# Four smaller transfers for the decays, and fewer, re-ordered rows for the reciprocals, in a gated linear-attention block

## The chip, the cores and the metric

The kernel runs on one core of one Trainium2 chip. A core has TensorE (PE, matrix products; its weight loads are listed as PEld), VectorE (DVE), ScalarE (ACT), GpSimd (POOL) and SyncE (SP), each with its own queue of instructions, and 16 DMA engines that all queues share. The metric is the device time of the program in microseconds (us), lower is better. The times shown are medians of runs. A profile is one execution, recorded by the hardware.

## The reference

The block has a linear attention with decays and a mixture of experts, each behind a layer norm whose scale and shift come from a condition `c`. There are 8 sequences of 2048 tokens, 256 features, 16 heads of 64, and 8 experts of which each token uses 2. Cut to what matters here:

```python
h = layernorm(x) * (1 + ca) + sa
q, k = elu(h @ Wq) + 1, elu(h @ Wk) + 1          # 16 heads of 64
v, a = h @ Wv, sigmoid(h @ Wa + ba + 2)          # one decay per head and token
S = a * S + k v^T                                # step by step over the tokens
z = a * z + k
o = (q S) / (q z + eps)                          # division by one number per head and token
x = x + ga * (o @ Wo)
h = layernorm(x) * (1 + cb) + sb
x = x + gb * mixture_of_two_experts(h)
```

Two quantities of this are what the change handles: the decays `a` as sums of logarithms per head and token, and the reciprocal of `q z + eps`, also one number per head and token.

## The kernel before

**Tiling.** A group is 256 tokens of one sequence; there are 64 groups. Each has two chunks of 128 tokens. Within a chunk the attention is computed as a masked matrix product (`Chunk.scores`, L486, and `Chunk.outputs`, L557); between chunks a state `S` is carried (`from_state`, `state`). All matrices are float32.

**Order.** The program order is written out by hand in a loop over the groups (L1158 on, under `manual_schedule`). One pass of it handles four groups at once: `here` has its attention outputs computed, `ahead` its keys, queries and decays, `coming` its norms and decay sums, `prev` its routing to the experts. Expert tiles (128 rows gathered for one expert: `load`, `turn`, `apply`, L846 to L891) are put in between by `expert_tiles`. Each engine does its instructions in that order, and a DMA queue issues in that order as well. Nearly all plain DMAs are issued by SP, on one queue (q1); POOL issues the indirect ones (L757 scatters rows to the experts' lists, L990 gathers the experts' results back).

**Decays.** `decays` (L343) makes for each head and token the running sum of the logarithm and its exponential, and stores both in DRAM (`led`, L374), as well as the decay itself (`ad`, L380). `chunk_decays` (L400) brings them back spread over the partitions: `dec` is a tile of 128 partitions by 16 heads by 128 tokens; each partition gets the same 16 x 128 numbers, 8 KB, in one DMA (L405). Then `el` gets half of the heads on each half of the partitions (`spread_pairs`, L392). POOL fills the part of `dec` above the diagonal with 1e30 (L409), and ScalarE makes exponentials of it, four heads between two other steps (L415). There are two `dec` buffers. The loop brings in chunk 0 of `ahead` early in a pass (L1212) and chunk 1 at its end (L1342).

**Reciprocals.** `denominators` (L444) multiplies the running sums `zz` (already times the queries) by a selecting matrix, so that head pair `2g+u`, half `q`, ends in row `32 g + 2 (q xor u) + u` of a PSUM tile of 128 rows by 256 tokens. 16 of the 128 rows are used. VectorE adds epsilon and takes reciprocals of all 128 (L457, L458). The whole tile is stored to DRAM (`rdd`, L460, 128 rows of 1 KB), and two DMAs (L465), one per half of the partitions, spread the used rows to 64 partitions each; of every block of 32 rows they read two neighbouring ones, 2 KB, so a partition's 8 KB come in four pieces. `Chunk.outputs` multiplies the product in PSUM by these (L577), for each `u` with a stride of two head pairs in `rb`. The denominators of `ahead` are made in the pass before the one that uses them: the store and the spread stand near the end of a pass, with `at` (the decays spread for the key sums, two DMAs of 512 KB, L395), `dec` of chunk 1 and `el` around them. In SP's order this stretch reads: `rdd`, `at` twice, `dec`, `rb` twice, `el` twice.

**Semaphores.** SP's DMAs use eight semaphores in turn, and each DMA first waits until the one that used its semaphore before, eight DMAs earlier, has landed.

Of the kernel before, what the change touches and what calls it, by code (L numbers as in the profile page):

```python
# [8 lines left out]
F32 = mybir.dt.float32  # L9
# [4 lines left out]
P = 128  # L14
C = 128
G = 2
GT = G * C
DH = 64
# [12 lines left out]
def adaln_block_kernel(  # L31
# [17 lines left out]
    nc = tc.nc  # L49
    B, N, D = x.shape  # L50
    F = wq.shape[1]
    H = F // DH
# [17 lines left out]
    dram = ctx.enter_context(tc.tile_pool(name="dram", bufs=3, space=bass.MemoryType.DRAM))  # L70
# [7 lines left out]
    def small_tile(name):  # L78
        return big_tile(name).rearrange("p i t -> p (i t)")
# [18 lines left out]
    for e in range(E):  # L98
# [6 lines left out]
        out=before, in_=before, compare_op=ALU.is_gt, fill=0.0, base=0,  # L105
# [45 lines left out]
    with tc.tile_pool(name="early", bufs=1) as early:  # L151
        wmod_sb = early.tile([P, KD, 4, D], F32, tag="wmod_sb", name="wmod_sb")
        for n in range(2):
            for k in range(KD):
                nc.scalar.dma_start(
                    out=wmod_sb[:, k, 2 * n : 2 * n + 2, :], in_=wmod_v[:, k, n, 0:2, :]
# [5 lines left out]
        for n, which in enumerate((0, 1, 3, 4)):  # L162
            t = cpool.tile([P, KD, B], F32, tag=f"modT{which}", name=f"modT{which}")
# [60 lines left out]
    for r in range(2 * G):  # L224
        row = (r // 2) * 32 + (r % 2) * NP
        nc.sync.dma_start(
            out=bias_a[row : row + NP, :],
            in_=ba.rearrange("(j q o) -> q j o", q=2, o=1)[r % 2],
# [7 lines left out]
    for u in range(2):  # L236
        for q in range(2):
            half = q ^ u
            nc.scalar.dma_start(
                out=wo_sb[half * DH : (half + 1) * DH].rearrange("p (g u) f -> p g u f", u=2)[  # L240
                    :, :, u, :
                ],
                in_=wo_v[u, q],
# [148 lines left out]
    def spread_pairs(dst, src):  # L392

        for q in range(2):
            nc.sync.dma_start(  # L395
                out=dst[q * DH : (q + 1) * DH],
                in_=src[q * NP : (q + 1) * NP].partition_broadcast(DH),
            )

    def chunk_decays(led, x, ch):  # L400

        tag = f"{x.tag}_{ch}"
        dec = wk2.tile([P, H, C], F32, tag="dec", name=f"dec_{tag}", bufs=2)
        el = wk2.tile([P, NP, C], F32, tag="el", name=f"el_{tag}", bufs=2)
        nc.sync.dma_start(out=dec, in_=led[0, ch * 32 : ch * 32 + H, :].partition_broadcast(P))  # L405
        yield dec, el
        spread_pairs(el, led[1, ch * 32 : ch * 32 + H, :])
        yield
        nc.gpsimd.affine_select(  # L409
            out=dec, in_=dec, compare_op=ALU.is_ge, fill=1e30, base=0,  # L410
            pattern=[[0, H], [1, C]], channel_multiplier=-1,
        )
        yield
        for h in range(H):
            nc.scalar.activation(  # L415
                dec[:, h, :], dec[:, h, :], AF.Exp, scale=-1.0, bias=x.lt[:, 0, ch, h : h + 1]
            )
            if h % 4 == 3:
                yield
# [24 lines left out]
    def denominators(qT, zz, tag):  # L444

        pd = small_tile(f"pd_{tag}")
        for u in range(2):
            for g in range(4):
                nc.tensor.matmul(  # L449
                    pd[g * 32 : (g + 1) * 32, :GT],  # L450
                    sel[:, u, :],
                    zz[:, 2 * g + u, :],
                    start=(u == 0),
                    stop=(u == 1),
                )
        rd = wk2.tile([P, GT], F32, tag="rd", name=f"rd_{tag}", bufs=1)
        nc.vector.tensor_scalar(rd, pd[:, :GT], ATTN_EPS, None, ALU.add)  # L457
        nc.vector.reciprocal(rd, rd)  # L458
        rdd = dram.tile([P, GT], F32, tag="rdd", name=f"rdd_{tag}")
        nc.sync.dma_start(out=rdd, in_=rd)  # L460
        yield

        rb = wk2.tile([P, NP, GT], F32, tag="rb", name=f"rb_{tag}", bufs=1)
        for half in range(2):
            nc.sync.dma_start(  # L465
                out=rb[half * DH : (half + 1) * DH].rearrange("p (g u) t -> p g (u t)", u=2),
                in_=rdd.rearrange("(g r) t -> g r t", r=32)[:, 2 * half : 2 * half + 2, :]
                .rearrange("g r t -> g (r t)")
                .partition_broadcast(DH),
            )  # L470
        yield rb

    class Chunk:
# [83 lines left out]
        def outputs(self, u):  # L557

            po = self.po[u]
            for i in range(NP // 2):  # L560
                for half in range(2):
                    j = 2 * i + u
                    q = half ^ u
                    h = 2 * j + q
                    nc.tensor.matmul(  # L565
                        po[half * DH : (half + 1) * DH, i, :],
                        self.v[:, h * DH : (h + 1) * DH],
                        self.dec[:, q * NP + j, :],
                        start=(self.S is None and i == 0),
                        stop=True,  # L570
                        skip_group_check=True,
                    )

            def pairs(t):
                return t.rearrange("p (g u) t -> p g u t", u=2)[:, :, u, :]

            nc.vector.tensor_mul(pairs(self.oT), po, pairs(self.group.rb[:, :, self.tok]))  # L577

        def decay_state(self):
            if self.last:  # L580
# [576 lines left out]
    with tc.manual_schedule():  # L1157
        for n in range(-2, total + 1):  # L1158
# [52 lines left out]
            if ahead:  # L1211
                dk = chunk_decays(ahead.led, ahead, 0)  # L1212
                ahead.dec_el[0] = next(dk)
                next(dk)
                kp = project(ahead.hT, "k", ahead.tag)
                ahead.kT = next(kp)
                zk = key_sums(ahead.kT, ahead.at, None if ahead.g == 0 else z, ahead.tag)
                zz, z = next(zk)
# [15 lines left out]
            if prev:  # L1234
# [4 lines left out]
                if n - 1 == dense_from:  # L1239

                    for e in range(0, E, 4):
                        for k in range(KD):
                            nc.sync.dma_start(
                                out=(wq_sb, wk_sb)[e // 4][:, k, :].rearrange(
                                    "p (e f) -> p e f", f=D
                                ),
                                in_=ew_d[e : e + 4, :, k, :].rearrange("e p f -> p e f"),
# [3 lines left out]
                else:  # L1251
                    u = unit_of[n - 1]
# [63 lines left out]
            if ahead:  # L1316
                dn = denominators(ahead.qT, zz, ahead.tag)
# [23 lines left out]
            if ahead:  # L1341
                ahead.dk = chunk_decays(ahead.led, ahead, 1)  # L1342
                ahead.dec_el[1] = next(ahead.dk)
                ahead.rb = next(dn)
                next(ahead.dk)
# [17 lines left out]
            if here and n < dense_from:  # L1363
                u = unit_of[n]
                if units[u] is None:
                    units[u] = Unit(u)
                nc.sync.dma_start(
                    out=units[u].xd[here.g * GT : (here.g + 1) * GT, :].rearrange(
                        "(c p) d -> p c d", p=P
                    ),  # L1370
                    in_=here.xt,
# [50 lines left out]
```

## Time and profile before

| | |
|---|---|
| median of 3 runs | 3899.13 us (3888.24 to 3919.3) |
| the profiled execution's own time | 3885.85 us |
| its span, first to last instruction | 3884.1 us |
| mean granted TensorE clock | 0.969 of full speed |
| bytes moved by DMA | 712.09 MB, mean 183 GB/s |
| of these on SP's queue | 625.52 MB in 313488 packets |
| `dec` (L405) | 128 DMAs of 1024 KB |
| `at` / `el` (L395) | 128 DMAs of 512 KB / 256 of 256 KB |
| `rdd` (L460) / `rb` (L465) | 64 DMAs of 128 KB / 128 of 512 KB |

A profile line of the waits names who waited, for whom, the total in us, how often, and the longest. A line of the timeline has start, duration, engine, source line, operation, output and inputs, shapes, how many instructions were merged, and in brackets the idle time before with what ended it. PE's idle time is what can be won as long as its work stays the same. A pass of the loop takes 50 us in the first sequence, 53 to 64 us in the middle, where expert tiles run beside the attention, and up to 84 us in the last sequence, in which more expert tiles are put between.

### The profile page before, as it was taken

What the parts mean: (1) busy time and instruction counts of PE and PEld (TensorE: products, weight loads), DVE (VectorE), ACT (ScalarE), POOL (GpSimd) and SP (SyncE); (2) the same over time, 40 slices, a digit from 0 to 9 for tenths busy, and PEclk for the clock granted to TensorE, in tenths of its full rate; (3) what the DMA queues carried; (4) which work ended last, traced back from release to release, by engine and by line L of the source; (5) the groups of instructions that cost most, each with busy time, mean ns of one, the idle gap of its engine ahead of it and who ended that gap; (6) DMA issues with size and microseconds to landing.
All of it is one profiled execution on the core that took longest, in us unless ns stands there. A gap on an engine that the chain in (4) does not pass through costs nothing.

```text
span 3884.1 us, 82134 instructions
## 1 busy us (share of the span) xinstructions
PE 3546.7 (91%) x28998; PEld 2742.2 (71%) x28998; DVE 2640.0 (68%) x6396; ACT 2083.2 (54%) x5423; POOL 1846.2 (48%) x1986
## 2 busy tenths in 40 slices
PE   5999999999999999999999998999999999788786
PEld 3777777777777777777777776777777777666665
DVE  3777777777667667667766767767767767556555
ACT  3555555655555645655555655555655555444442
POOL 1444443443555454454545546445455444444554
PEclk9999999999999999999999999999999999989898
DMA  6444457666676666676576676576576576666766
GB/s 188 130 122 133 133 148 194 196 176 170 196 217 175 186 179 193 182 216 185 161 222 188 181 192 188 172 209 190 171 209 195 164 205 180 200 190 197 212 199 189
DMA packets 347404, 712.09 MB, mean 183 GB/s; under 512 B 43736, under 2 KB 212968, under 8 KB 322416
## 3 DMA queue, kind: packets, MB, share of 16 engines
q1 hardware_dynamic: 313488, 625.52, 57.5%
q0 software_dynamic: 27264, 74.49, 5.6%
q10 hardware_dynamic: 6240, 6.84, 0.6%
q8 instruction: 229, 3.75, 0.4%
q14 instruction: 183, 1.50, 0.1%
HBM read 577.29 MB, written 132.53 MB: 183 GB/s over the span
## 4 chain that ended last, share of the span: by engine, by line
PE 64%; DVE 15%; ACT 7%; issue 6%; DMA 3%; POOL 2%; SPq 0%; another core or an unknown queue 0%; DVEq 0%; ACTq 0%; POOLq 0%
PE pv L528 10%; PE pw L615 9%; PE pq L326 7%; PE pk L326 7%; PE po L565 6%; PE py L886 5%; PE sc L492 4%; PE ps L599 3%; PE po L548 3%; DVE at L433 3%; PE pd L449 2%; PE pk L511 2%; DMA xg<-xrows 2%; POOL at L1154 2%; ACT dec L415 2%
## 5 line engine op out<-in xcount | busy, mean ns | idle before, releaser
L415 ACT ACTIVATE dec<-dec,lt 128x128 f32<-128x128 f32 x2048 | 628.5, 389 | 14.2 <-POOL dec L409 14.2
L1154 POOL TENSOR_TENSOR at<-at,qT 128x512 f32<-128x512 f32 x256 | 326.1, 1285 | 579.2 <-DVE rmark L715 401.6
L326 PE MATMUL pk<-hT_a,wk_sb 128*128 128x256 f32 x2048 | 512.8, 395 | 5.0 <-issue 4.7
L326 PE MATMUL pq<-hT_a,wq_sb 128*128 128x256 f32 x2048 | 482.2, 389 | 13.2 <-DVE kT L338 12.5
L615 PE MATMUL pw<-wo_sb,oT 128*128 128x256 f32 x2048 | 478.0, 388 | 4.7 <-DVE oT L577 4.7
L528 PE MATMUL pv<-wv_sb,hT_a 128*128 128x512 f32 x1024 | 472.3, 604 | 2.5 <-DVE yg L890 2.3
L326 PEld LDWEIGHTS pq<-hT_a,wq_sb 128*128 128x128 f32 x2048 | 392.0, 194 | 75.4 <-DVE kT L338 19.4
L875 ACT ACTIVATE xgT<-pxt,modT,modT 128x128 f32<-128x128 f32 x622 | 245.0, 447 | 358.4 <-PE pxt L870 336.6
L615 PEld LDWEIGHTS pw<-wo_sb,oT 128*128 128x128 f32 x2048 | 393.5, 195 | 59.2 <-DVE oT L577 5.5
L326 PEld LDWEIGHTS pk<-hT_a,wk_sb 128*128 128x128 f32 x2048 | 381.1, 196 | 70.3 <-issue 13.3
L886 PE MATMUL py<-we,xgT 128*128 128x256 f32 x1244 | 348.4, 405 | 62.1 <-ACT xgT L875 28.3
L409 POOL TENSOR_SCALAR_AFFINE_SELECT dec<-dec 128x2048 f32<-128x2048 f32 x128 | 256.9, 2007 | 266.4 <-DMA dec<-led 201.8
L577 DVE TENSOR_TENSOR oT<-po,rb 128x512 f32<-128x512 f32 x256 | 173.1, 690 | 296.2 <-PE po L565 119.2
L433 DVE TENSOR_TENSOR_SCAN at<-at,z,kT 128x256 f32<-128x256 f32 x448 | 353.7, 830 | 2.0
L501 DVE TENSOR_TENSOR dec<-sc,dec 128x512 f32<-128x512 f32 x512 | 327.3, 682 | 36.8 <-PE sc L492 35.2
L528 PEld LDWEIGHTS pv<-wv_sb,hT_a 128*128 128x128 f32 x1024 | 189.8, 192 | 216.7 <-issue 174.2
L620 POOL TENSOR_TENSOR xt<-xt,dx 128x256 f32<-128x256 f32 x128 | 94.3, 737 | 480.2 <-DVE dx L619 479.9
L565 PE MATMUL po<-dec,v 128*64 128x128 f32 x4096 | 272.3, 278 | 36.1 <-issue 26.0
L886 PEld LDWEIGHTS py<-we,xgT 128*128 128x128 f32 x1244 | 227.5, 200 | 103.6 <-ACT xgT L875 35.7
L492 PE MATMUL sc<-qT,kT 64*128 64x128 f32 x4096 | 298.1, 286 | 0.1
L492 PEld LDWEIGHTS sc<-qT,kT 64*128 64x128 f32 x4096 | 250.1, 188 | 63.0 <-issue 62.8
L336 ACT ACTIVATE lowk<-pk 128x512 f32<-128x512 f32 x256 | 152.3, 595 | 257.0 <-PE pk L326 218.8
(199 smaller groups left out, 6208.2 us busy)
## 6 DMA issues: line engine op xcount, KB each, us to landing
dec<-led SPq DMA_DIRECT2D x128, 1024.0 KB
we<-ew_d SPq DMA_DIRECT2D x311, 384.0 KB
at<-ad SPq DMA_DIRECT2D x128, 512.0 KB
el<-led SPq DMA_DIRECT2D x256, 256.0 KB
rb<-rdd SPq DMA_DIRECT2D x128, 512.0 KB
xg<-xrows SPq DMA_DIRECT2D x311, 128.0 KB
yrows<-yg SPq DMA_DIRECT2D x311, 128.0 KB
xt<-in_L_attn_x_dram SPq DMA_DIRECT2D x64, 256.0 KB
```

The costliest lines, as they stand in the source:

```text
L326: nc.tensor.matmul(pp[:, j * GT : (j + 1) * GT], w[:, k, (jj + j) * P : (jj + j + 1) * P], hT[:, k, :], start=(k == 0), stop=(k == KD - 1),)
L409: nc.gpsimd.affine_select(out=dec, in_=dec, compare_op=ALU.is_ge, fill=1e30, base=0, pattern=[[0, H], [1, C]], channel_multiplier=-1,)
L415: nc.scalar.activation(dec[:, h, :], dec[:, h, :], AF.Exp, scale=-1.0, bias=x.lt[:, 0, ch, h : h + 1])
L433: nc.vector.tensor_tensor_scan(zz[:, j, :], at[:, j, :], kT[:, j, :], 0.0 if z is None else z[:, j : j + 1], ALU.mult, ALU.add,)
L492: nc.tensor.matmul(sc[q][:, i, :], self.kT[rows, half * 4 + i, self.tok], self.qT[rows, half * 4 + i, self.tok], start=True, stop=True,)
L501: nc.vector.tensor_mul(w4, sc[q], w4)
L528: nc.tensor.matmul(pv, self.hT[:, k, self.tok], wv_sb[:, k, i * 512 : (i + 1) * 512], start=(k == 0), stop=(k == KD - 1),)
L565: nc.tensor.matmul(po[half * DH : (half + 1) * DH, i, :], self.v[:, h * DH : (h + 1) * DH], self.dec[:, q * NP + j, :], start=(self.S is N ...
L615: nc.tensor.matmul(pw[:, :D], self.oT[:, j, :], wo_sb[:, j, :], start=(j == 0), stop=(j == NP - 1))
L875: nc.scalar.activation(self.xT[:, k, :], pt[:, k * P : (k + 1) * P], AF.Identity, bias=modT[3][:, k, b : b + 1], scale=modT[4][:, k, b : b ...
L886: nc.tensor.matmul(py[:, :D], self.xT[:, k, :], self.w[:, k, :], start=(k == 0), stop=(k == KD - 1))
L1154: nc.gpsimd.tensor_mul(zz[:, part, :], zz[:, part, :], ahead.qT[:, part, :])
```

## The change

Three places change; the order of the other work stays as it is on every engine.

- `dec` is brought in by four DMAs of four heads each instead of one of 16 heads. A partition's part in one DMA is 2 KB instead of 8 KB. The consumer on POOL still takes the whole tile.
- Of the reciprocals only the 16 used rows are stored, by four DMAs of four rows each: `r`, `r+32`, `r+64`, `r+96` of the tile go to `rdd[r]`. So the 8 rows for one half of the partitions lie together in DRAM, 8 KB.
- The two spreading DMAs read these 8 KB in one piece. The tile `rb` is therefore ordered by `u` first and `g` second, and the multiply takes four neighbouring blocks instead of every second one.

```diff
-        nc.sync.dma_start(out=dec, in_=led[0, ch * 32 : ch * 32 + H, :].partition_broadcast(P))
+        for h in range(0, H, 4):
+            nc.sync.dma_start(
+                out=dec[:, h : h + 4, :],
+                in_=led[0, ch * 32 + h : ch * 32 + h + 4, :].partition_broadcast(P),
+            )
         yield dec, el
...
-        rdd = dram.tile([P, GT], F32, tag="rdd", name=f"rdd_{tag}")
-        nc.sync.dma_start(out=rdd, in_=rd)
+
+        rdd = dram.tile([4, 4, GT], F32, tag="rdd", name=f"rdd_{tag}")
+        for r in range(4):
+            nc.sync.dma_start(out=rdd[r], in_=rd[r :: 32, :])
         yield
...
-                out=rb[half * DH : (half + 1) * DH].rearrange("p (g u) t -> p g (u t)", u=2),
-                in_=rdd.rearrange("(g r) t -> g r t", r=32)[:, 2 * half : 2 * half + 2, :]
-                .rearrange("g r t -> g (r t)")
+                out=rb[half * DH : (half + 1) * DH].rearrange("p j t -> p (j t)"),
+                in_=rdd[2 * half : 2 * half + 2]
+                .rearrange("u g t -> (u g t)")
                 .partition_broadcast(DH),
...
-            nc.vector.tensor_mul(pairs(self.oT), po, pairs(self.group.rb[:, :, self.tok]))
+            nc.vector.tensor_mul(
+                pairs(self.oT), po, self.group.rb[:, 4 * u : 4 * u + 4, self.tok]
+            )
```

## The prediction

> **What bounds the kernel now.** I read the page's busy table first, then the waits of TensorE, then one group in order of time with the DMA rate beside it.
>
> ```profile
> PE 3546.7 (91%) x28998; PEld 2742.2 (71%) x28998; DVE 2640.0 (68%) x6396; ACT 2083.2 (54%) x5423; POOL 1846.2 (48%) x1986
> ...
> q1 hardware_dynamic: 313488, 625.52, 57.5%
> ```
>
> TensorE is busy for 3546.7 of 3884.1 us. 337 us are left, and only those can be won by a change that moves no matmul. SP's queue (q1) fills the DMA engines for 57.5% of the span, so I asked which of TensorE's idle time is a transfer's. From the waits of TensorE, whole span:
>
> ```profile
> PE pxt L870 <- DMA xg<-xrows: 51.2, 7, 11.6
> ...
> PE po L565 <- issue: 26.0, 49, 1.1
> PE ps L599 <- issue: 24.2, 44, 1.2
> ```
>
> One DMA wait matters, 51.2 us in 7 places; 42.7 us of it are four waits between 3340 and 3745 us (the same view of that stretch). It is for `xg`, which this change doesn't touch but which stands behind `dec` and `rb` on SP's queue. So I looked at where the queue is full. Windows of one group (columns: stretch, length, busy us and instructions of PE, PEld, DVE, ACT, POOL, granted clock, DMA share, GB/s):
>
> ```profile
> 1541.00:1547.00 6.00, 6.00 (x62) 5.14 (x59) 3.45 (x10) 2.96 (x8) 3.04 (x5) 1.00 1.03 217
> 1547.00:1550.00 3.00, 3.00 (x40) 2.59 (x37) 2.34 (x5) 0.00 (x0) 1.81 (x3) 1.00 0.96 319
> 1550.00:1556.00 6.00, 6.00 (x56) 3.53 (x56) 4.91 (x12) 2.65 (x7) 2.77 (x2) 1.00 1.06 221
> 1557.00:1561.00 4.00, 1.54 (x17) 0.98 (x14) 0.00 (x0) 2.14 (x8) 2.62 (x4) 0.98 1.07 389
> 1564.00:1567.00 3.00, 3.00 (x17) 2.67 (x16) 0.33 (x1) 1.58 (x4) 2.83 (x2) 0.96 1.05 393
> ```
>
> Once a group there is a burst with a DMA share of 1.0. By the sizes of the packet records 1541 to 1547 is `at` (8 KB packets to 64 partitions at a time), then `dec` (8 KB, all 128), 1550 to 1556 is `rb` (2 KB, 64 partitions), and 1564 to 1567 is the other chunk's `dec` alone. `at` and `rb` run at 220 GB/s, `dec` at 390. TensorE goes on through the burst (6.00 of 6.00). From 1557 to 1561, when `rb` and `el` are through, it has 1.54 of 4.00; four row gathers by POOL are out then.
>
> **What the late landing of rb costs now.** In another group, in order of time:
>
> ```profile
> 921.93 1.99 PE L326 MATMUL pk<-hT_a,wk_sb 128*128 128x256 f32 x8
> 923.48 0.34 SPq L853 DMA_DIRECT2D xg<-xrows  x1
> 923.55 1.29 DVE L577 TENSOR_TENSOR oT<-po,rb 128x512 f32<-128x512 f32 x2 [4.93 <-DMA rb<-rdd]
> 923.76 0.60 PE L299 MATMUL pn_f<-ident,lnn_f 128*128 128x128 f32 x4
> 924.03 0.58 ACT L336 ACTIVATE lowk<-pk 128x512 f32<-128x512 f32 x1
> 924.20 1.89 PE L326 MATMUL pk<-hT_a,wk_sb 128*128 128x256 f32 x8
> ```
>
> VectorE stands 4.93 us for `rb`, and TensorE runs on without a gap (5.00 of 5.00 busy in both windows from 920 to 930). `rb` has slack of several us before TensorE feels it, so a shift of a us either way in it is worth little.
>
> **The change part by part.**
>
> *Stores of the reciprocals.* 64 stores of 128 rows become 256 of 4 rows. SP pays three more issues a group: `rdd`'s median is 331 ns, and the nearest row for a few short rows, `ad` (16 rows), 503 ns. I take 400, so +1.2 us (1.0 to 1.5). These stand ahead of `at`, and `at` opens the burst: its first packet starts 1.3 us after its issue, as the last weight packets end, so nothing covers the delay. 124 fewer rows of 1 KB at 46 ns over 16 engines free 0.36 us a group, but ahead of the point where SP is now late, so I count 0 (bounds 0 and -0.36).
>
> *rb in rows of 8 KB.* 512 packets of 2 KB a group become 128 of 8 KB. The nearest row is `at`, which has the new form exactly. From the starts of the packet records I took the rate in the middle of each transfer, over 56 groups: `at` 240 GB/s, `rb` 199, `dec` 358 (medians). So 1.05 MB falls from 5.3 to 4.4 us: -0.9 us a group. Here a rule speaks against it. The Trainium skill ("SBUF — State Buffer", Door 1: the DMA port swizzle) says that a range of 64 partitions reaches only 8 of the 16 DMA ports, whatever the rows. That fits the 220 against 390 GB/s; by it alone rb would gain nothing. I take -0.9 and keep 0 as the other end.
>
> *dec by four transfers.* The bytes are the same; 16,384 packets of 8 KB become 65,536 of 2 KB. The nearest row is `gt`, rows of 2 KB spread to 128 partitions: 84 ns a packet. Four are 336 ns, against a median of 334 for an 8 KB packet of `dec` in the burst. So about +0.1 us a transfer; at the other end, if 2 KB rows lose here what rb loses against `at` (a sixth), 2.9 us become 3.5: +0.6. The rule against it is the skill's "DMA: Bandwidth & Descriptors", Rules for kernel authors (1 MiB or more a transfer) and its Anatomy section (about 2 us fixed for each DMA, fitted for another queue kind). By it three more DMAs would cost 6 us, 128 times 6 = 768 us. But `at`'s two halves land 6.7 and 8.5 us after the first's issue (landing records at 1540 us): the second is 2.1 us behind, and half a MB at 240 GB/s is 2.2. Fixed costs overlap in the queue. I take the row.
>
> SP pays three more issues of 406 ns (the median of `dec`), 1.2 us for each chunk. In the burst they lie behind `at`'s 4.4 us of transfer; `rb` and `el`, now issued at 1542 and 1543.6, would be issued some 2.5 us later, and their packets start only at 1549 and 1554. In the other chunk `dec`'s own 2.7 us cover `el`. Without this cover it would be 128 times 1.2 = 157 us.
>
> *Waits moved.* Each of SP's DMAs uses one of eight semaphores in turn and waits for the transfer eight before it. With three more stores and three more `dec`, the third and fourth `dec` wait for the first stores (now landing 3.0 us after issue, median; by then SP is about there), `el` waits for `at`, and the next `xg` load for the third `dec` instead of `at`'s second half. Queued behind are `yrows`, `xg`, `we`, `xd`. At 1549.69 `xg` was issued and landed only at 1558.9, behind `rb` and `el`: 3 us later at issue is hidden by those 6 us. POOL's select (L409) waits for four semaphores instead of one, three more events of 17 to 28 ns: under 10 us on an engine that is 48% busy, so 0.
>
> *The multiply (L577).* Same shape, 690 ns, another stride between blocks of 128: 0.
>
> **Sum.** `dec` lands 1.3 us later (start of the burst, +0.1); `rb`, `el` and `xg` 1.2 - 0.9 + 0.1 = +0.4 us later. Who pays: TensorE in the 7 waits for `xg`, 2.8 us; the first group, where store and spread follow each other with nothing beside, +1; elsewhere the slack above. That is +4 us: 3890 against the profiled execution's 3885.85 (its span 3884.1 and 1.8 around it), which is 13 us under the median of the runs, 3899.13. So 3903.
>
> **Rivals.**
>
> *The late burst is passed on (slower).* Store issues cost 500 ns like `ad` (+1.7), rb gains nothing (the port rule), dec +0.2: everything behind lands 1.9 us late, in 62 groups. If TensorE pays half, 62 x 0.95 = 59 us: 3958; in full 118 us: 4017. For it: `rb` already holds up VectorE in many groups. Against it: the 4.93 us above without a gap. It decides once `rb` is late by more than the slack, roughly 3 us beyond now, or in every group where `S` and `kT` queue behind L577 on VectorE. At dec's worst end (+0.6 for each) it is nearer.
>
> *The gathers fall into a freer queue (faster).* POOL's four gathers follow L409, which follows `dec`. In the groups at 1419, 1883 and 2812 they start after `el` is through and TensorE's broken stretches at L565 and L599 are absent; in most others they start 2.5 to 5 us before, and TensorE loses about 2 us. With dec 1.3 us later and el's end about where it was, the overlap shrinks. If 17 of some 35 such stretches go, 34 us, and with them the halved clock that follows (about 1.5 us each, 25 us), it is 3840. Against it: most overlaps are longer than the shift.
>
> *It does nothing.* rb stays at its port rate and SP's issues are covered: 3899. It lies within the forecast.
>
> **Numbers.** Forecast 0.60 (3880 to 3930), slower rival 0.25, faster rival 0.15. About 1%, 39 us, is what a measurement of this kernel can tell from no change (its three runs span 3888 to 3919). The range cuts each rival in about half: 3840 to 3960. Faster by over 1% 0.15, within 0.62, slower 0.23.
>
> **What would show it.** In the profile after: rb's stretch at 240 GB/s instead of 199; `at`'s issue about 1.2 us further behind the last `we`; three more SP rows per store and per dec, 330 to 500 ns each; the wait of L870 for `xg` still near 51 us; dec's packets at 84 ns. I would be wrong if 2 KB rows of dec, read by all engines at once, ran at rb's rate, if the four gathers' stretches changed in number, or if SP became the last to arrive in the late groups with three expert tiles in a row.

## The result and the profile after

The changed kernel takes 3920.06 us (median, 3904.73 to 3935.64), the kernel before, beside it, 3891.72 us (3876.24 to 3919.3). The ratio is 1.0077, with a 95% interval of 1.0062 to 1.0092: 28 us slower, which is within 1%. The profiled executions are 18.9 us apart: 3903.0 against 3884.1 us of span. The prediction said 3903 us, 4 us slower. The number lies in the range, but the loss is seven times the sum that was worked out, so most of it is not in that sum. That it still falls into the range is luck: the range is 50 us wide, and the 3903 were reckoned from a median of 3899 us for the kernel before.

The busy table and SP's queue of the changed kernel:

```profile
PE 3545.8 (91%) x28998; PEld 2739.2 (70%) x28998; DVE 2666.4 (68%) x6396; ACT 2082.1 (53%) x5423; POOL 1847.6 (47%) x1986
...
q1 hardware_dynamic: 337040, 618.20, 58.2%
```

TensorE does the same work in the same time (3546.7 before). VectorE is busy 26.4 us longer, although the change gives it not one instruction more and the edited multiply costs 690 ns before and after. So some of its operations were stretched. Three rows of the waits before that the prediction had no use for:

```profile
POOL dec L409 <- DMA dec<-led: 201.8, 50, 13.3
...
DVE oT L577 <- DMA rb<-rdd: 50.5, 16, 10.4
...
PE pq L326 <- DVE kT L338: 12.5, 36, 1.0
```

and what answers to them, and to the wait for `xg`, in the changed kernel:

```profile
POOL dec L413 <- DMA dec<-led: 251.2, 70, 18.3
...
DVE oT L583 <- DMA rb<-rdd: 80.3, 24, 13.1
...
PE pxt L878 <- DMA xg<-xrows: 58.4, 7, 13.5
...
PE pq L326 <- DVE kT L338: 29.2, 40, 1.4
```

POOL waits 49 us longer for `dec`, VectorE 30 us longer for `rb`, and TensorE 17 us longer for `kT`, which VectorE makes. Its wait for `qT` at the transposes of the keys, which VectorE makes as well, grew by 10 us (15.0 to 24.8). The wait for `xg`, where the prediction put most of its loss, grew by 7 us. Another loss of TensorE is spread thin: from the first score product of group 1 to that of group 9, eight groups without expert tiles, the span is 401.0 us before and 408.3 after, about 1 us a group; another 4.6 us are lost ahead of group 1.

By stretches the pair's 18.9 us are 12.5 ahead of group 10, and 9.3 from group 57 on, where the waits for `xg` stand. Groups 10 to 56 are 2.9 us shorter in this pair (2692.8 and 2689.9 us), although the wait for `kT` grew in them.

One of these early groups, in order of time. Before (SP's issues first; then VectorE and POOL):

```profile
319.30 0.34 SPq L460 DMA_DIRECT2D rdd<-rd  x1
320.12 0.85 SPq L395 DMA_DIRECT2D at<-ad  x2
...
336.19 0.69 DVE L577 TENSOR_TENSOR oT<-po,rb 128x512 f32<-128x512 f32 x1 [1.64 <-PE po L565]
...
339.84 2.37 POOL L1048 TENSOR_TENSOR el<-el,qT 128x1024 f32<-128x1024 f32 x1
...
341.93 1.47 DVE L433 TENSOR_TENSOR_SCAN at<-at,z,kT 128x256 f32<-128x256 f32 x2
```

The same group after, where TensorE reaches it 8.6 us later:

```profile
327.92 2.14 SPq L466 DMA_DIRECT2D rdd<-rd  x4
330.29 1.12 SPq L395 DMA_DIRECT2D at<-ad  x2
...
347.61 1.29 DVE L583 TENSOR_TENSOR oT<-po,rb 128x512 f32<-128x512 f32 x2 [4.45 <-DMA rb<-rdd]
...
350.56 3.46 DVE L437 TENSOR_TENSOR_SCAN at<-at,z,kT 128x256 f32<-128x256 f32 x2
350.65 2.83 POOL L1056 TENSOR_TENSOR el<-el,qT 128x1024 f32<-128x1024 f32 x1
```

`at` is issued 2.37 us after the first store in place of 0.82. The whole burst slides, and 16.9 us after the store VectorE had its multiply L577 waiting for TensorE; now, at 19.7, it waits for `rb`. The update of `S` behind it is late on VectorE, and so is POOL's product with that `S`; POOL's multiply of `el` then starts 22.7 us after the store in place of 20.5. VectorE's scan starts when it did, 22.6 us after the store, but now it meets that multiply: two scans take 3.46 us in place of 1.47. The routing products and the rest of the projection behind it come late on TensorE. In groups 1 to 6 the longest scan took 0.8 to 1.2 us before, and takes 1.5 to 2.8 in the changed kernel.

### The profile page after: what moved, and what is told of

It is laid out like the page before. It is cut to its first block, busy times and chain, and to the rows that moved or that the text cites. A ratio compares the mean times of both kernels' runs of the same rounds, so it can differ in the third digit from the quotient of the medians.

```text
span 3903.0 us, 83109 instructions
## 1 busy us (share of the span) xinstructions
PE 3545.8 (91%) x28998; PEld 2739.2 (70%) x28998; DVE 2666.4 (68%) x6396; ACT 2082.1 (53%) x5423; POOL 1847.6 (47%) x1986
## 4 chain that ended last, share of the span: by engine, by line
PE 63%; DVE 16%; ACT 7%; issue 6%; DMA 5%; POOL 1%; SPq 1%; another core or an unknown queue 0%; DVEq 0%; ACTq 0%
PE pv L534 10%; PE pw L623 9%; PE pq L326 7%; PE pk L326 7%; PE po L571 6%; PE py L894 6%; PE sc L498 4%; DVE at L437 3%; PE ps L607 3%; PE po L554 3%; PE pk L517 2%; PE pd L453 2%; ACT dec L419 2%; DMA xg<-xrows 2%; POOL at L1162 1%
## 5 line engine op out<-in xcount | busy, mean ns | idle before, releaser
L419 ACT ACTIVATE dec<-dec,lt 128x128 f32<-128x128 f32 x2048 | 628.6, 389 | 16.9 <-POOL dec L413 16.6
L628 POOL TENSOR_TENSOR xt<-xt,dx 128x256 f32<-128x256 f32 x128 | 93.5, 731 | 470.7 <-DVE dx L627 470.6
L571 PE MATMUL po<-dec,v 128*64 128x128 f32 x4096 | 266.7, 277 | 26.9 <-issue 17.2
L1056 POOL TENSOR_TENSOR el<-el,qT 128x1024 f32<-128x1024 f32 x120 | 286.0, 2383 | 5.5
```

What stands on the lines that cost most here:

```text
L419: nc.scalar.activation(dec[:, h, :], dec[:, h, :], AF.Exp, scale=-1.0, bias=x.lt[:, 0, ch, h : h + 1])
L571: nc.tensor.matmul(po[half * DH : (half + 1) * DH, i, :], self.v[:, h * DH : (h + 1) * DH], self.dec[:, q * NP + j, :], start=(self.S is N ...
L1056: nc.gpsimd.tensor_mul(el, el, x.qT[:, :, ch * C : (ch + 1) * C])
```

## The experiments

Two readings were open. **Theory A**: the three extra stores ahead of `at` delay the burst, and this is passed on through `rb` and VectorE. **Theory B**: the loss comes from the decays, their rows of 2 KB and the semaphores that move with them (the changed kernel's `el` waits 129.9 us for `at` to land, which it didn't before).

The kernels ran in three sets of four, each set on one chip with the kernel before beside it. The chips are not alike: the kernel before takes 3752 us in the first set, 3887 in the second and 3754 in the third, against 3892 in the comparison above. Every ratio is against the kernel before of the same set.

### First set: the parts (before: 3752.06 us)

**The decays by four, alone.** Edit: the first block of the change's diff, nothing else.

> Only the decays by four transfers of four heads; the store and the spread of the reciprocals as before. Theory A (the three extra stores of reciprocals ahead of `at` delay the burst, and that is passed on through rb and VectorE): this part costs next to nothing, ratio to before 0.999 to 1.0015 (-4 to +6 us). Theory B (the decays' rows of 2 KB and the extra semaphores in turn, with el waiting for `at`, carry the loss): +20 to +28 us, ratio 1.005 to 1.007, and the SP wait for `at` at el's issue is there as in the changed kernel.

Measured: 3778.59 us, ratio 1.008 (1.0063 to 1.0097). Theory A fails here: the decays by themselves cost 26 us (30 by the ratio).

**The reciprocals, alone.** Edit: the rest of the change's diff.

> Only the reciprocals' part: four stores of four rows, rb in rows of 8 KB, the multiply that goes with it; the decays by one transfer. Theory A: nearly the whole loss, +20 to +28 us, ratio 1.005 to 1.007, with TensorE about 1 us longer in each of the first eight groups, and `at` issued 1.2 to 1.8 us later after the first store. Theory B: within 0.15% of before (-5 to +5 us), or faster by the gain of rb's 8 KB rows.

Measured: 3759.2 us, ratio 1.003 (1.0017 to 1.0043). It costs 7 us (11 by the ratio), less than half of what theory A asks, more than theory B allows. The early groups are as theory A has them: 407.2 us for the eight.

**Four stores, nothing else.**

```diff
-        nc.sync.dma_start(out=rdd, in_=rd)
+        for r in range(4):
+            nc.sync.dma_start(out=rdd[r * 32 : (r + 1) * 32], in_=rd[r * 32 : (r + 1) * 32])
```

> The kernel before with its one store of 128 rows cut into four stores of 32 rows: the same bytes and packets, rb in rows of 2 KB and the decays by one transfer as before. It prices three more store issues ahead of `at` alone. Theory A: +25 to +40 us (as the reciprocals' part, without the 0.9 us a group that rb's larger rows give back), ratio 1.006 to 1.010. Theory B: within 0.15% of before.

Measured: 3759.52 us, ratio 1.0029 (1.0015 to 1.0042), the same as with rb in rows of 8 KB. So the stores' issues carry the cost of this part. The two are not quite alike: stores of 32 rows are issued faster, and `at` follows the first of them by 1.94 us in place of 2.35 (0.56 with one store). Larger rows of `rb` give back no more than that difference.

**The changed kernel with `at` ahead of the stores.**

```diff
         nc.vector.reciprocal(rd, rd)
+        yield
         rdd = dram.tile([4, 4, GT], F32, tag="rdd", name=f"rdd_{tag}")
...
                 coming.at = spread_decays(ad, coming.tag)
+            advance(dn)
```

> The changed kernel with one thing moved: the two transfers of `at` are issued ahead of the four stores of reciprocals, so that the stores stand between `at` and the decays, inside `at`'s transfer. Theory A: the burst starts as early as before or earlier, and the loss goes: -10 to +6 us against before, ratio 0.997 to 1.0015. Theory B: the decays are still in four transfers, the loss stays: +18 to +28 us, ratio 1.005 to 1.007.

Measured: 3771.54 us, ratio 1.0063 (1.0047 to 1.0079). The early groups are cured (401.3 us for the eight), the whole isn't. Both causes are there: the stores cost in the early groups, the decays somewhere else.

Where, can be read from the starts of the score products. Each length is of one profiled execution, the last column the waits view's row for TensorE's `pq` on `kT`:

```
                                      groups 1-8   groups 10-56   pq waits for kT
reciprocals alone                       407.2        2567.9           28.0
four stores alone                       403.7        2565.8           25.9
decays by four alone                    402.3        2592.5           43.2
changed kernel, at ahead of stores      401.3        2586.9           54.5
```

With decays by four the 47 groups from 10 to 56 are 19 to 27 us longer, some 0.5 us each. Between the first and the third row 25 us are lost there: TensorE's wait for `kT` at `pq` takes 16 of them, and 8.5 are time lost to a halved clock (17.1 and 25.6 us). (The groups before them have no expert tiles.) Why: one of these groups, the same in two kernels. POOL's, VectorE's and TensorE's rows, with the reciprocals alone, `dec` by one transfer; TensorE began this group at 1523.9:

```profile
1546.88 2.01 POOL L409 TENSOR_SCALAR_AFFINE_SELECT dec<-dec 128x2048 f32<-128x2048 f32 x1
...
1548.34 0.69 DVE L362 TENSOR_TENSOR ae<-ae,ay 64x128 f32<-64x128 f32 x1 [1.73 <-ACT ae L361]
...
1549.51 0.28 DVE L367 TENSOR_TENSOR left<-le 64x128 f32<-64x128 f32 x1
...
1552.83 1.26 DVE L338 SCALAR_TENSOR_TENSOR kT<-pk,lowk 128x512 f32<-128x512 f32 x2
...
1553.55 2.64 PE L326 MATMUL pq<-hT_a,wq_sb 128*128 128x256 f32 x11 [0.25 <-DVE kT L338]
```

With the decays by four, where it began at 1525.3:

```profile
1549.11 0.28 DVE L362 TENSOR_TENSOR ae<-ae,ay 64x128 f32<-64x128 f32 x1 [1.11 <-ACT ae L361]
...
1549.56 2.08 POOL L413 TENSOR_SCALAR_AFFINE_SELECT dec<-dec 128x2048 f32<-128x2048 f32 x1 [1.25 <-PE pk L326]
...
1549.87 1.91 DVE L367 TENSOR_TENSOR left<-le 64x128 f32<-64x128 f32 x1
...
1554.81 1.26 DVE L338 SCALAR_TENSOR_TENSOR kT<-pk,lowk 128x512 f32<-128x512 f32 x2
...
1555.53 2.64 PE L326 MATMUL pq<-hT_a,wq_sb 128*128 128x256 f32 x11 [0.85 <-DVE kT L338]
```

In the first, POOL starts its select without having waited; it runs out under a stretch where VectorE waits for ScalarE anyway, and only the end of it holds up `ae`. In the second the last of the four transfers lands at 1549.33 and the select starts behind it (its row names `pk`, on which the select doesn't depend), 1.3 us later within the group, and VectorE's next operation on two tensors in SBUF, `left`, takes 1.91 us in place of 0.28: it ends about when the select ends. The routing chain behind it, `kT`, and TensorE's `pq` follow 0.6 us later. The Trainium skill names the mechanism ("SBUF — State Buffer", Who interferes with whom): a VectorE operation with two inputs in SBUF contends with a GpSimd operation that reads SBUF, and the second to issue is blocked until the first is done. The trace agrees: `left` 0.28 or 1.91 us, while VectorE's product of decays and scores, which has one input in PSUM, takes 0.68 us under a select as elsewhere.

The select is late because the transfer is. The first chunk's `dec` meets a queue with little else in it. Over 46 groups, from the first issue to landing it takes a median of 5.7 us by one transfer and 8.5 us by four (in the comparison above: 6.2 and 8.6). POOL is busy until 30.4 us before the next group's scores. By one transfer (the reciprocals alone) `dec` has landed 31.2 us before them, by four it lands 30.0 before them, and the select starts 0.7 us later in the median. In 26 of the 47 groups it now starts later than 30.0 us before the scores, against 14 and 9 with one transfer. The number of late selects is no measure of the cost, though: when both parts were run again (third set below), it was 20 against 9, with a larger loss.

### Second set: which chunk, and the select (before: 3887.1 us)

**Theory C** is that chain: lone transfer, late select, VectorE held, `kT` late. **Theory D**: more issues, packets and semaphores cost alike in either chunk.

**First chunk only, second chunk only.**

```diff
+        for h in range(0, H, 4 if ch == 0 else H):
+            w = 4 if ch == 0 else H
+            nc.sync.dma_start(
+                out=dec[:, h : h + w, :],
+                in_=led[0, ch * 32 + h : ch * 32 + h + w, :].partition_broadcast(P),
+            )
```

(and `ch == 1` for the other).

> The kernel before with four transfers for the decays of each group's first chunk only (the transfer that has the queue nearly to itself); the second chunk's by one. Theory C (alone in the queue, four transfers of 256 KB land 2.7 us later after the first issue than one of 1 MB; POOL's select, no longer covered, starts later, holds up VectorE's two-input operations of the routing chain, and TensorE then waits for kT): the whole loss of the decays' part, +18 to +28 us, ratio 1.005 to 1.0075, with TensorE's wait for kT at pq near 43 us. Theory D (three more issues, more packets and more semaphores in turn, in either chunk alike): half of it, +9 to +14 us, ratio 1.0025 to 1.004.

> The kernel before with four transfers for the decays of each group's second chunk only (the one that is queued behind `at` in the burst, where el then waits for `at` to land); the first chunk's by one. Theory C: next to nothing, -6 to +5 us, ratio 0.9985 to 1.0015, TensorE's wait for kT at pq as with one transfer, near 26 us. Theory D: half of the loss of the decays' part, +9 to +14 us, ratio 1.0025 to 1.004.

Measured: first chunk 3891.61 us, ratio 1.0011 (0.9995 to 1.0027); second chunk 3891.31 us, ratio 1.0016 (1.0001 to 1.0031). Theory C's price fails here: 18 to 28 us were asked of the first chunk, at most 11 lie in its interval; nor does the time tell the two chunks apart, and theory D's 9 to 14 us for each lies just inside both intervals at its low end. The late selects go where C puts them, 11 with the first chunk by four against 6 with the second (6 before), and so does TensorE's wait for `kT` at `pq`: 18.9 us, 11.4, and 12.5 in the profile of before. But it is 6 us and not 17. TensorE also waits for `kT` at `py`, in the expert tiles: 13.9 us with the first chunk by four, 21.0 with the second, 11.9 before. With both rows added, the two chunks can't be told apart (32.8 and 32.4, against 24.4). So the chain is seen where only the first chunk is cut, but that it is the loss isn't shown on this chip. On these chips the groups are longer (2692.8 us for groups 10 to 56 in the profile of before), and in that profile the first chunk's `dec` is issued 40.1 us ahead of the next scores and lands 33.5 ahead, 3 us before POOL is free; where the kernel before takes 3752 us it is issued at 37.1 and has under 1 us of cover. Most of the slower landing is hidden here. In the profile of the changed kernel 17 selects are late.

**The select in four.**

```diff
-        nc.gpsimd.affine_select(
-            out=dec, in_=dec, compare_op=ALU.is_ge, fill=1e30, base=0,
-            pattern=[[0, H], [1, C]], channel_multiplier=-1,
-        )
+        for h in range(0, H, 4):
+            nc.gpsimd.affine_select(
+                out=dec[:, h : h + 4, :], in_=dec[:, h : h + 4, :], compare_op=ALU.is_ge,
+                fill=1e30, base=0, pattern=[[0, 4], [1, C]], channel_multiplier=-1,
+            )
```

with the decays by four, and with them by one:

> The decays by four transfers in both chunks, and POOL's select cut into four of four heads, each of which needs its own transfer alone; the reciprocals as before. Theory C: three quarters of the select run as the pieces land, and a select holds VectorE for at most 0.6 us in place of 2.0; at least half of the loss goes: -8 to +10 us against before, ratio 0.998 to 1.0027. Theory D: the transfers are what they were, +20 to +30 us, ratio 1.005 to 1.008, or more by six more POOL instructions a group.

> The kernel before with POOL's select cut into four of four heads, all behind the one transfer. Theory C: VectorE's time under a running select (about 105 us over what the same operations take elsewhere) falls to under half, TensorE's wait for kT at pq falls below 20 us: -4 to -20 us against before, ratio 0.995 to 0.999. If the hold by POOL does not matter to TensorE: -3 to +4 us.

Measured: with the decays by four 3841.05 us, ratio 0.9883 (0.9859 to 0.9907), 46 us faster than before; with one transfer 3883.63 us, ratio 0.9993 (0.998 to 1.0006). TensorE's wait for `kT` at `pq` falls to 4.8 and 8.5 us, that at `py` to 3.4 and 4.8. The first is far past what theory C asked, and theory D fails: the transfers are the same ones. Under one transfer the shorter selects alone gain nothing that can be told, although VectorE's extra time under them falls from 99 us in the profile of before to 76 (the time of each operation that overlaps a select, less the median of the same operation elsewhere). So it is not the shorter hold alone but the pieces: each select needs only its own transfer.

Of the 46 us, 8 are the wait for `kT` at `pq`, and 8.5 that at `py`. In groups 10 to 56 TensorE's gaps of over 0.12 us add up to 106.0 us in place of 134.8 in the profile of before, and the time lost to a halved clock (length of each stretch at half clock, times a half) 32.4 in place of 54.6. These come and go with the short stalls around POOL's gathers, of which this chip has many. That the select in four brought this about, and not its new place in time, isn't shown.

### Third set: once more, and together (before: 3753.63 us)

**Theory E**: what a late `dec` costs depends on how near VectorE's chain already is to TensorE's need on that chip. **Theory F**: the two chunks together cost more than their sum. The first two kernels are those of the first set again.

> The decays by four transfers alone, in both chunks, once more, beside the reciprocals' part alone on the same chip. The first time it was +26 us (ratio 1.008) where the kernel before takes 3752 us; its halves, where the kernel before takes 3887 us, were +4 and +6 us. Theory E (what the late decays cost depends on how close VectorE's routing chain already is to TensorE's next need in a group of that chip): +5 to +15 us if the kernel before is near 3890 us here, +24 to +34 us if it is near 3750. Theory F (the two chunks together cost more than their sum): +20 us or more wherever it runs.

> The reciprocals' part alone (four stores, rb in rows of 8 KB), once more. Theory E: the rest of the changed kernel's +30 us: +14 to +24 us if the kernel before is near 3890 us here, +8 to +14 us (the first time +11) if it is near 3750. Theory F: +4 to +10 us wherever it runs.

Measured: decays 3789.15 us, ratio 1.0094 (1.0077 to 1.0111); reciprocals 3762.88 us, ratio 1.0021 (1.0013 to 1.0029). Both repeat. In groups 10 to 56 of this pair of profiles the decays by four are 32 us longer, 23 of them the wait for `kT` at `pq`; at `py` it is about the same (14.5 and 13.2 us). As the kernel before takes 3754 us here again, they don't tell E from F by time: neither part was run whole on a chip where it takes 3890. What speaks for E is the cover counted above, 3 us on the one kind of chip and under 1 on the other.

The pair shows how the lone transfer is slow. Windows of 1 us, the second and third after the first issue of one such `dec` (columns as in the prediction: the last three are granted clock, DMA share, GB/s). One transfer:

```profile
1655.34:1656.34 1.00, 1.00 (x7) 0.87 (x6) 0.68 (x4) 1.00 (x4) 0.00 (x0) 1.00 1.16 472
1656.34:1657.34 1.00, 1.00 (x6) 0.90 (x5) 0.69 (x4) 1.00 (x5) 0.00 (x0) 1.00 0.97 410
```

Four transfers:

```profile
1658.59:1659.59 1.00, 1.00 (x7) 0.87 (x6) 1.00 (x3) 0.00 (x0) 0.00 (x0) 1.00 0.90 236
1659.59:1660.59 1.00, 1.00 (x6) 0.89 (x5) 0.93 (x5) 0.00 (x0) 0.00 (x0) 1.00 0.89 174
```

Over groups 10 to 56 the median share between 2 and 3.5 us after the issue is 1.01 with one transfer and, in four profiles, 0.68 to 0.76 with four, and `dec` moves at 409 to 417 and 152 to 172 GB/s. So the rate falls further than the share, as the rows show too. Most packets of 2 KB still take 84 ns, but some are far longer: the mean in this stretch is 138 to 148 ns, where a packet of 8 KB has 323. Four packets for one thus take 1.7 to 1.8 times as long, and the idle engines add a factor of 1.3 to 1.5. The issues aren't the limit: four of them, 0.47 us apart, offer 256 KB each, 550 GB/s. Why the packets are long there is open. In the burst, where the queue is full, the changed kernel's `dec` moves at 358 GB/s.

**The changed kernel with the select in four** (the same edit, on the changed kernel):

> The changed kernel with POOL's select cut into four of four heads, each needing one of the four transfers. If the select by pieces is what made the decays by four transfers 46 us faster than before instead of slower, it does so here too, less what the four stores cost: -20 to -40 us against before, ratio 0.990 to 0.995. If that gain was an accident of where the gathers fell: -10 to +28 us.

Measured: 3751.54 us, ratio 0.9991 (0.998 to 1.0001). It isn't the 20 to 40 us faster that were asked; it lies in the range that was set for an accident of the gathers, and so the 46 us of the second set don't repeat as a gain over before. But on this chip, where the decays alone lose 35 us and the reciprocals 9, the two together with the select in four lose nothing. (The changed kernel itself was not run beside it; that it would lose the sum of the two is assumed.) TensorE's waits for `kT` at `pq`, one row of each; the reciprocals alone, the decays by four alone, and this kernel:

```profile
PE pq L326 <- DVE kT L338: 29.8, 42, 2.2
```

```profile
PE pq L326 <- DVE kT L338: 51.8, 45, 2.4
```

```profile
PE pq L326 <- DVE kT L338: 14.6, 23, 2.7
```

and what a select can do to `left` in the last two, by its tile (min, median, max ns): decays by four alone, then with the select in four:

```profile
L367 DVE TENSOR_TENSOR left<-le x64: 282/283/2127, 46.8 to 3524.5; 64x128 f32<-64x128 f32 x64
```

```profile
L367 DVE TENSOR_TENSOR left<-le x64: 282/283/766, 47.5 to 3488.0; 64x128 f32<-64x128 f32 x64
```

The hold is at most 0.5 us now in place of 1.8. Groups 10 to 56 take 2553.5 us, against 2568.2 with `dec` by one transfer and 2600.0 by four. The stores' cost stays: 406.0 us for groups 1 to 8.

**One store of 16 rows.**

```diff
-                    pd[g * 32 : (g + 1) * 32, :GT],
-                    sel[:, u, :],
+                    pd[:32, :GT],
+                    sel[:, u, g, :],
                     zz[:, 2 * g + u, :],
-                    start=(u == 0),
-                    stop=(u == 1),
+                    start=(u == 0 and g == 0),
+                    stop=(u == 1 and g == 3),
...
-        rdd = dram.tile([P, GT], F32, tag="rdd", name=f"rdd_{tag}")
-        nc.sync.dma_start(out=rdd, in_=rd)
+        rdd = dram.tile([H, GT], F32, tag="rdd", name=f"rdd_{tag}")
+        nc.sync.dma_start(out=rdd, in_=rd[:H])
```

> A version: the decays by four transfers, POOL's select in four, and the 16 reciprocals put into 16 adjoining rows by the selector matmul, so that one store of 16 rows takes the place of four (or of one of 128), with rb in rows of 8 KB. With no extra issue ahead of `at` and rb at the higher rate: at least as good as the decays and the select in four, -45 to -60 us, ratio 0.984 to 0.9885. If four stores cost nothing, it equals the changed kernel with the select in four.

Measured: 3834.08 us, ratio 1.0215 (1.0194 to 1.0235): 80 us slower. The expectation left TensorE out. The group of the selecting products, in the kernel before (in its own profile) and here:

```profile
L449 PE MATMUL pd<-at,sel 128*32 128x256 f32 x1024 | 93.5, 388 | 23.1 <-POOL at L1154 19.4 <-POOL mark L756 1.9 <-DVE dec L501 1.3
```

```profile
L455 PE MATMUL pd<-at,sel 128*32 128x256 f32 x1024 | 234.5, 382 | 19.4 <-POOL at L1163 19.3
```

The same number of products with the same mean, but 234.5 us busy in place of 93.5: with results in four blocks of 32 rows the products had run more than four at a time (1024 of 388 ns are 397 us, in 93.5), into one block fewer than two (391 us in 234.5). The 128-row tile with 16 used rows, which looks wasteful at the store, was what made the products cheap. Whether one store of 16 rows would have paid is left open by this.

## Why the prediction was right and where it was wrong

*dec by four transfers: the step that failed.* "About +0.1 us a transfer; at the other end +0.6" holds for the burst, where the changed kernel's `dec` runs at 358 GB/s. For the first chunk it is +2.4 to +2.8 us from first issue to landing. The row taken was the duration of a packet, 84 ns, which is right as a median; but with nothing else queued the mean was 138 to 148 ns early in the transfer, and the engines were busy for 0.7 of it. The rule that was weighed and put aside (the Trainium skill, "DMA: Bandwidth & Descriptors", Rules for kernel authors: 1 MiB or more a transfer) pointed the right way; its fixed price, 768 us in all, was far too high.

*"In the other chunk dec's own 2.7 us cover el."* That names who waits for `el`, not who waits for `dec`. The cover of `dec` was a lone `dec` that landed 0.5 to 3 us before POOL was free, by the chip. And "three more events, so 0" for the select counted its waiting and not what a later select holds up. The changed kernel's POOL waits 49 us longer for `dec`, and VectorE is held where its operation with two inputs in SBUF meets the later select. On the chips where it was run whole this part costs 26 and 35 us.

*The stores ahead of `at`.* Each costs 478 ns in place of the 400 taken; `at` is issued 1.5 us later in groups 1 to 8 where +1.2 (1.0 to 1.5) was said; over all groups it is 1.9 (medians 0.51 and 2.37 us after the first store), more than the slower rival's 1.7. (The stores also drop 112 rows a group, not 124; that term was counted as 0.) The mechanism, "nothing covers the delay", is right. The step behind it is wrong: "`rb` has slack of several us". The group from which this was read has expert tiles between; groups 1 to 8 have none, `rb` there lands 8.9 us after the group's first score product (median of the eight, before), where the product that it multiplies is done at 9.0; there is no slack, and the delay goes through: 12 us up to group 9 in the profiled pair. For the part by itself it is 9 us in both profiles (6 with four stores and nothing else), against the profile of before, which is of a slower chip. That is the slower rival's mechanism, confined to a sixth of its 62 groups.

*rb in rows of 8 KB.* -0.9 us a group was taken, with 0 as the other end by the port rule. The rate in the middle of the transfer is 208 GB/s in the changed kernel, against 201 by the same measure before; four stores with and without the larger rows cost the same. The other end was nearly right here; the 240 GB/s of `at` did not carry over.

*The waits moved, 0.* `el` does wait for `at` now, 129.9 us in all. With the second chunk alone by four, which has that wait, the cost is 0 to 12 us.

*xg:* +2.8 us said, +7.2 measured in the pair. *The multiply:* 690 ns before and after, as said.

*The faster rival* (gathers into a freer queue): TensorE's wait at `po` fell from 26.0 to 17.2 us, that at `ps` stayed (24.2 and 24.5). Too little to win.

How the 28 us divide on a chip where the kernel before takes 3890 stays open. In the profiled pair the early part is 12 us longer and the last groups 9, 7 of them the wait for `xg`. The wait for `kT` is 16.7 us longer too, but the groups in which it stands are not: other stalls fell (at `po` by 9 us), and so did the time lost to a halved clock (54.6 to 51.2 us in groups 10 to 56). The pair differs by 18.9 us and the medians by 28. The two halves of the decays gave 4 us each there, and neither has the longer wait for `qT` (8.6 and 10.1 us, against 24.8 in the changed kernel); whether that comes with the reciprocals' part or only with both together is open too.

## What to carry to other kernels

Before a transfer is cut in pieces, ask of each place where it is issued whether the queue is full there: in a full queue the pieces ran here at the rate of the whole, in a nearly empty one these landed 2.7 us late, and the median duration of a packet, 84 to 88 ns, doesn't tell the two apart. If pieces must be used, try cutting the consumer too, so that it starts on the first piece: here that took the loss away, though it made a gain on one chip only. Short instructions of POOL also hold up VectorE for less, 0.5 us in place of 1.8. A slack is read in the barest group, the one with nothing between, not in the one that happens to show a long wait without a gap.

## What the runs showed of the hardware

- Four broadcasts of 256 KB in an otherwise quiet queue keep the DMA engines 0.68 to 0.76 busy between 2 and 3.5 us after the issue, with packets of 138 to 148 ns in the mean (84 in the median); one of 1 MB keeps them at 1.01. Why is open.
- POOL's select of 2.0 us stretches a 0.28 us operation of VectorE to as much as 2.1 us when both inputs of that are in SBUF.
- Eight selecting products into four blocks of 32 rows take 1.5 us a group (93.5 / 64), into one block 3.7 us (234.5 / 64).
- The same kernel takes 3752 us on one chip and 3887 us on another. In groups 10 to 56 of the profiles the second kind loses more to short stalls of TensorE at the products of `po` and `ps` and the projection `pk` (58.6 against 5.2 us) and to a halved clock (54.6 against 22.2 us; before against the reciprocals alone). An experiment's size is therefore only good beside a run of the kernel before on the same chip.
